# Routing a whole batch row at once, the spread of y about its first channel, and the output matrix's sums inside the first expert, in a fused attention and mixture-of-experts kernel

## The chip, the core and the metric

The kernel runs on one core of a Trainium2 chip. The core's engines each have their own in-order instruction queue: TensorE (PE) multiplies matrices, VectorE (DVE), ScalarE (ACT) and GpSimd (POOL) do elementwise work, and SyncE (SP) issues most DMAs. An engine waits for another through semaphores. SBUF holds the operands, PSUM the products. The metric is the time of one execution in microseconds (us) on the device; lower is better.

## The reference, cut to what is computed

```
x : (4, 1024, 1024) f32, all weights f32
xn  = layernorm(x)                              # no gain, no bias
# attention part
q, v = xn @ Wq, xn @ Wv
s_t  = lam * s_{t-1} + v_t                      # scan over the 1024 tokens, lam per head
y    = layernorm(q * s) * ln_g + ln_b
A    = (y * silu(xn @ Wg)) @ Wo
# experts: 64 experts, the 8 best per token, 128 places per expert
p    = softmax(xn @ router.T)
w, i = top_k(p, 8);  w = w / sum(w)
per expert e, for the first 128 tokens that chose it:
     h = silu(xg @ w1[e].T) * (xg @ v1[e].T)    # 384 wide
     M[token] += w * (h @ w2[e])
out  = x + A + M
```

Tokens are taken for an expert in the order of their position, the four batch rows interleaved.

## The kernel before

**Stages.** `attn_and_routing` works through the four batch rows of 1024 tokens; then `Experts.run` goes through the 64 experts and weaves the 16 products with `Wo` in between them. Within a row, channels lie on the partitions (a "channel block" c is 128 channels; y(c), c = 0 to 7, is one such block of 1024 tokens), and for each m = 0 to 3 there is a product for the states v (`states`), then one for the queries q (`queries`), and after these eight, four products for the gate g (`gates`). Each makes two channel blocks, m and m+4.

**One product.** `steps` (L130 to L175) makes the two channel blocks for all 1024 tokens with seven multiplications of half blocks where the plain way needs eight; each is four matmuls of 128x512. `left_sums` (L49) forms the needed sums of the weights, `right_sums` (L57) those of the right operand: T3, T1, T2, T4 at L61, L64, L66 and L68, in this order; T1 is written over B12. The seven parts lie in PSUM banks of the kinds a, b and c, two of each. ACT copies three of them to SBUF (`sc1`, `sc5`, `sc2`, L148), DVE adds at L160, L169 and L172. Two further banks, t and r, exist once each. In `product` (L178) the last multiplication of one product is left over and is done after two steps of the next one (`before`), and whatever is handed in as `late` comes after five of them.

**Order.** A scheduler chooses each engine's instruction order from the program and its dependences. `in_order` (L79) holds program order on the engines that are named; `keep_in_program_order` pins single instructions. Row 0's preparation is pinned on all engines, experts 0 to 2 on DVE alone (L976).

**Router.** `scored` (L468) makes the logits of half a row (512 tokens): the eight channel blocks of xn are split into two groups of four that are multiplied side by side, 64 experts on partitions 0 to 63 and 64 to 127 of one bank. ACT copies the bank, and `folded` (L487) adds both groups and turns tokens onto the partitions with four matmuls against a constant matrix `fold`. `route` (L501) takes, for 512 tokens, the maximum, the eight best (one MAX8 and one MATCH_REPLACE for each 128 tokens), the softmax over them, and stores the weights to `wtab` in DRAM. Row 0's two halves are scored at the end of its preparation and routed as the function `left` within the first product; the first half of row b+1 is scored and routed after row b's queries m=2, the second before the gates m=3. `take` (L527) turns the selection of each half to experts on partitions (transposes to `sT`, bank r, before the queries m=0) and picks the best 128 tokens for each expert in 16 rounds that are spread over the row.

**Spread of y.** The layernorm of y needs sums over 1024 channels, that is, across partitions and over eight blocks. `sum1` adds the blocks and `sum2` their squares on POOL; a 128x512 matmul with a constant matrix `mean_w` then averages over partitions (`all_channels`). To keep the squares small, the kernel first finds a shift per token from the first two blocks, y(0) and y(4): `find_shift` runs one such matmul per half row inside the product after queries m=0 (as `late`), and `less_shift` subtracts the shift from each block, squares it on ACT (L628 and next) and adds on POOL (L630, L631). `find_spread` runs inside the gates m=0, as `late`: mean matmuls, copies on ACT, the mean's square, the variance matmuls, root and reciprocal.

**Experts.** `hidden` (L883) multiplies the 128 gathered tokens by w1 and v1 (16 matmuls of 128x384) and makes `act`; `output` (L899) turns act (`hpt`, three transposes), copies it (`hT`, L906) and multiplies by w2 (six matmuls of 128x512, `y`). `turned` makes the next expert's transposed tokens `xgT`. `load_wo` (L931) loads the four blocks of Wo and forms their sums, in the program before expert 0; row 3's last gate products are then still running.

Of the kernel before, what the change touches and what calls it, by code (L numbers as in the profile page):

```python
# [8 lines left out]
F32 = mybir.dt.float32  # L9
# [223 lines left out]
def attn_and_routing(  # L233
# [45 lines left out]
    begun = {}  # L279
    first_logits = []  # L280

# [19 lines left out]
    def prep_first():  # L301
# [61 lines left out]
        with in_order(tc):  # L363
            for n in range(4):
                load_x(n)
            load_w(0, (0, 1))
            load_x(4)
            load_x(5)
            load_w(1, (0, 1))
            load_x(6)  # L370
            load_x(7)
            nc.sync.dma_start(out=r_sb, in_=router)
            for w in range(2):
                load_w(w, (2, 3))
            for n in range(3):
                moments(tiles[n], tables[n], f"{n}")
                root_of(n)
                if n > 0:
                    norm(n - 1)
            for n in range(2 * NM):  # L380
                if n > 0:
                    if n + 2 < 2 * NM:
                        moments(tiles[n + 2], tables[n + 2], f"{n + 2}")
                        root_of(n + 2)
                    if n + 1 < 2 * NM:
                        norm(n + 1)
                turn(n)
                for work in then.get(n, ()):
                    work()
            left_sums(nc.vector, ws[0])  # L390
            sums(0)
            left_sums(nc.vector, ws[1])
            halves = [scored(0, h, "rt"[h]) for h in range(2)]
            first_logits.extend(folded(0, h, halves[h], "rt"[h]) for h in range(2))
        begun.update({w: (banks[w, 0], banks[w, 1]) for w in range(2)})
# [71 lines left out]

    def scored(b, h, bank="r"):  # L468


        blocks = quarters[b]
        two = pools.bank(bank, [P, SH], f"lg2_{b}_{h}")
        for k in range(KH):
            for i in range(2):
                nc.tensor.matmul(  # L475
                    two[i * E : (i + 1) * E, :],
                    lhsT=r_sb[:, i * KH + k, :],
                    rhs=blocks[f"B{i + 1}{h + 1}"][:, k, :],
                    start=(k == 0),
                    stop=(k == KH - 1),  # L480
                    tile_position=(0, i * E),
                )
        both = scratch.tile([P, SH], F32, tag="sc", name=f"lgs_{b}_{h}")
        nc.scalar.copy(both, two)
        return both

    def folded(b, h, both, bank="r"):  # L487

        lg = pools.bank(bank, [P, NM, E], f"lg_{b}_{h}")
        for j in range(NM):  # L490
            nc.tensor.matmul(
                lg[:, j, :],
                lhsT=both[:, j * P : (j + 1) * P],
                rhs=fold,
                start=(j == 0),
                stop=(j == NM - 1),
                skip_group_check=True,
            )
        return lg

    def route(b, h, lg):  # L501

        wide = [P, NM, E]
        mx = small.tile([P, NM], F32, tag="mx", name=f"mx_{b}_{h}")
        nc.vector.tensor_reduce(mx, lg, AX.X, ALU.max)
        sh = scratch.tile(wide, F32, tag="sc", name=f"sh_{b}_{h}")
        nc.vector.tensor_tensor(sh, lg, mx.unsqueeze(2).to_broadcast(wide), ALU.subtract)
        nc.vector.tensor_scalar(sh, sh, EXP_MIN, None, ALU.max)
        sel = small.tile(wide, F32, tag="sel", name=f"sel_{b}_{h}")
        for j in range(NM):  # L510
            top = small.tile([P, K], F32, tag="top", name=f"top_{b}_{h}_{j}")
            nc.vector.max(top, sh[:, j, :])
            nc.vector.match_replace(sel[:, j, :], top, sh[:, j, :], TAKEN)
        nc.vector.tensor_tensor(sel, sel, sh, ALU.is_lt)
        nc.scalar.activation(sh, sh, AF.Exp)
        nc.vector.tensor_tensor(sh, sh, sel, ALU.mult)
        sm = small.tile([P, NM], F32, tag="mx", name=f"sm_{b}_{h}")
        nc.vector.tensor_reduce(sm, sh, AX.X, ALU.add)
        nc.vector.reciprocal(sm, sm)
        nc.vector.tensor_tensor(sh, sh, sm.unsqueeze(2).to_broadcast(wide), ALU.mult)  # L520
        r0 = b * S + h * SH
        nc.gpsimd.dma_start(
            out=wtab[r0 : r0 + SH, :].rearrange("(j p) e -> p j e", p=P), in_=sh
        )
        sels[b, h] = sel

    def take(b):  # L527

        cur = one.tile([E, C + S], F32, tag="cur", name=f"cur_{b}")
        for h in range(2):  # L530
            sT = pools.bank("r", [E, SH], f"sT_{b}_{h}")
            for j in range(NM):
                nc.tensor.transpose(
                    sT[:, j * P : (j + 1) * P], sels[b, h][:, j, :], ident
                )
# [46 lines left out]
    def batch_row(b, left):  # L582
# [7 lines left out]

        shift = mean = ys[2][:, 2, :]
        sum1 = one.tile([P, S], F32, tag="sum1", name=f"sum1_{b}")
# [10 lines left out]

        def states(m, left, late):

# [3 lines left out]
            def then(c21):  # L609
# [5 lines left out]
                nc, pools, weights(b, 0, m), quarters[b],  # L615
                lo[:, H0], lo[:, H1], hi[:, H1], then, left, f"v_{b}_{m}", late,
                begun.get(0) if b == 0 and m == 0 else None,
# [3 lines left out]
        def queries(m, lo, hi, left):  # L621
            def less_shift():
                for i, c in enumerate((m, m + KH)):
                    nc.vector.tensor_tensor(y(c), y(c), shift, ALU.subtract)  # L624
                    if m == 0 and i == 0:
                        nc.scalar.activation(sum2, y(c), AF.Square)
                        continue
                    sq = line.tile([P, S], F32, tag="line", name=f"sq_{b}_{c}")  # L628
                    nc.scalar.activation(sq, y(c), AF.Square)
                    nc.gpsimd.tensor_tensor(sum2, sum2, sq, ALU.add)  # L630
                    nc.gpsimd.tensor_tensor(sum1, y(0) if m == 0 else sum1, y(c), ALU.add)  # L631

            def find_shift():
                for h, cols in enumerate((H0, H1)):
                    ps = all_channels(sum1, h, f"sh_{b}_{h}")
                    nc.scalar.activation(shift[:, cols], ps, AF.Copy, scale=float(NM))
                less_shift()

            def then(c21):
                nc.vector.tensor_tensor(y(m + KH, H0), c21, hi[:, H0], ALU.mult)  # L640
                nc.vector.tensor_tensor(y(m), y(m), lo, ALU.mult)
                nc.vector.tensor_tensor(y(m + KH, H1), y(m + KH, H1), hi[:, H1], ALU.mult)
                if m == 0:
                    nc.gpsimd.tensor_tensor(sum1, y(0), y(KH), ALU.add)
                else:
                    less_shift()

# [4 lines left out]
            )  # L652
            return left, find_shift if m == 0 else None

        def find_spread():

            for h, cols in enumerate((H0, H1)):
                ps = all_channels(sum1, h, f"mean_{b}_{h}")
                nc.scalar.copy(mean[:, cols], ps)
            rstd = one.tile([P, S], F32, tag="sum1", name=f"rstd_{b}")  # L660
            nc.scalar.activation(rstd, mean, AF.Square)
            for h, cols in enumerate((H0, H1)):
                ps = all_channels(sum2, h, f"var_{b}_{h}")
                nc.vector.tensor_tensor(rstd[:, cols], ps, rstd[:, cols], ALU.subtract)
            nc.scalar.activation(rstd, rstd, AF.Sqrt, bias=eps)
            nc.vector.reciprocal(rstd, rstd)
            spread.append(rstd)
# [31 lines left out]

        late = None  # L700
        taking = take(b)
        for m in range(NM):
            lo, hi, left = states(m, left, late)
            if b == 0 and m == 0:
# [7 lines left out]
            next(taking)  # L712
            left, late = queries(m, lo, hi, left)
            next(taking)
            if b + 1 < B:
                if m == 1:
                    prep(b + 1, 0)
                elif m == 2:
                    load_turned(b + 1, 0)
                    route(b + 1, 0, folded(b + 1, 0, scored(b + 1, 0)))  # L720
            if m == NM - 1:
# [8 lines left out]
        for m in range(NM):  # L730
            if m == 0 and b + 1 < B:
                prep(b + 1, 1)
            if m == NM - 1 and b + 1 < B:
                load_turned(b + 1, 1)
                route(b + 1, 1, folded(b + 1, 1, scored(b + 1, 1)))
                sums(b + 1)
# [80 lines left out]

    def left():
        for h in range(2):
            route(0, h, first_logits[h])  # L820

    for b in range(B):
# [4 lines left out]
class Experts:  # L827
# [103 lines left out]
    def load_wo(self):  # L931
        for name, (i, o) in zip(("B11", "B21", "B22", "B12"), BLOCKS):
            self.wo_b[name] = self.pools.block(f"wo_{name}")
            load_block(self.nc, self.wo_b[name], self.wo, i, o * SH, SH)
        right_sums(self.nc.vector, self.wo_b, lambda n: self.pools.block(f"wo_{n}"))

# [27 lines left out]
    def run(self):  # L964
        units = B * NM
        gated = self.load_gated(0)
# [7 lines left out]
        for e in range(E):  # L974

            kept = [mybir.EngineType.DVE] if e < 3 else []  # L976
            with in_order(self.tc, kept):
# [3 lines left out]
                if e + 1 < E:  # L981
                    self.turn = self.turned(e + 1)
                if before is not None:
                    self.output(*before)
# [57 lines left out]
```

## Time and profile before

| | us |
|---|---|
| median of three runs | 2669.09 (2668.46 to 2669.94) |
| the profiled execution, its time | 2671.9 |
| its span, first to last instruction | 2670.1 |
| mean granted TensorE clock | 0.997 of full speed |

Some more rows of the page, from its table of the costliest groups. Each gives line, engine and operation, destination and sources with partitions x elements, the count, then busy time in total and the mean in ns of one, then the idle time ahead of them and what ended it.

```profile
L890 PE MATMUL h<-w,xgT 128*128 128x384 f32 x2048 | 672.2, 486 | 0.7 <-issue 0.7
...
L906 DVE COPY hT<-hpt 128x384 f32<-128x384 f32 x64 | 35.6, 557 | 724.5 <-PE hpt L905 724.5
...
L631 POOL TENSOR_TENSOR sum<-sum,y 128x1024 f32<-128x1024 f32 x24 | 56.9, 2373 | 205.2 <-DVE y L624 205.2
```

A f32 matmul shows as two records that overlap in the pipeline, so the mean of one is longer than the distance between their starts; prices are best taken from start to start. A POOL instruction that follows something of DVE shows long idle time, which costs nothing where POOL is not what ends a stage.

The experts take the second half of the span. The attention part ends at about 1255 us, where the first expert's matmuls are already mixed with row 3's last gate product.

### The profile page before, as it was taken

Reading aid. Unit: us, or ns where it says so; the run is one execution under the profiler, and the core shown is the slowest. Engines: PE = TensorE matmul, PEld = TensorE weight load, DVE = VectorE, ACT = ScalarE, POOL = GpSimd, SP = SyncE. Lnnn points to the kernel's source line nnn. Section 1 sums busy time; section 2 is a strip of 40 time slices with the busy share of each in tenths; the row PEclk is TensorE's granted clock in tenths of the full one; section 3 lists DMA queues with packets and bytes.
Section 4 is the critical chain, followed back from the end, with each engine's and each line's share of the span. In section 5 each row is a group of like instructions: output and inputs, shape, how many; then the busy total and the mean of one; then the engine's idle time right before and its main releaser. Section 6 shows DMA issues by size and latency. Waiting matters only on the chain.

```text
span 2670.1 us, 18675 instructions
## 1 busy us (share of the span) xinstructions
PE 2642.0 (99%) x6981; PEld 1272.4 (48%) x6981; DVE 1082.8 (41%) x1426; ACT 330.8 (12%) x492; POOL 737.5 (28%) x655
## 2 busy tenths in 40 slices
PE   9999999999999999999999999999999999999997
PEld 5444444444444444444555555555555555555554
DVE  7945676464943676373222212222122221222221
ACT  4213112131212211121000000000000000000000
POOL 1453312121122102132333323333233332333321
PEclk9999999999999999999999999999999999999999
DMA  6555534443335432326889888898888988889876
GB/s 236 194 182 194 193 107 144 179 156 110 123 110 210 166 116 83 145 98 239 296 284 305 283 274 284 285 304 283 274 284 284 305 283 273 284 286 303 270 272 181
DMA packets 122474, 592.95 MB, mean 222 GB/s; under 512 B 15872, under 2 KB 52736, under 8 KB 89360
## 3 DMA queue, kind: packets, MB, share of 16 engines
q1 hardware_dynamic: 81488, 448.03, 46.1%
q0 software_dynamic: 40464, 143.72, 19.9%
q8 instruction: 55, 0.90, 0.1%
q14 instruction: 35, 0.29, 0.0%
q10 hardware_dynamic: 432, 0.01, 0.0%
HBM read 483.67 MB, written 124.81 MB: 228 GB/s over the span
## 4 chain that ended last, share of the span: by engine, by line
PE 95%; DVE 3%; DMA 1%; issue 0%; ACT 0%; POOL 0%; SPq 0%; POOLq 0%; DVEq 0%; ACTq 0%
PE h L890 25%; PE y L911 12%; PE pa_o L137 8%; PE pa_g L137 8%; PE pa_v L137 7%; PE pa_q L137 7%; PE pc_o L137 4%; PE pc_q L137 4%; PE pc_g L137 4%; PE pc_v L137 4%; PE pb_g L137 2%; PE pb_o L137 2%; PE pb_v L137 2%; PE pb_q L137 2%; PE lg L475 1%; PE hpt L905 1%
## 5 line engine op out<-in xcount | busy, mean ns | idle before, releaser
L890 PE MATMUL h<-w,xgT 128*128 128x384 f32 x2048 | 672.2, 486 | 0.7 <-issue 0.7
L890 PEld LDWEIGHTS h<-w,xgT 128*128 128x128 f32 x2048 | 388.9, 190 | 286.1 <-issue 33.6
L857 POOL DMA_INDIRECT xg<-rows,tables x256 | 252.6, 987 | 669.4 <-DVE xgT L875 603.7
L911 PE MATMUL y<-w,hT 128*128 128x512 f32 x768 | 343.6, 597 | 1.6 <-DVE hT L906 1.6
L906 DVE COPY hT<-hpt 128x384 f32<-128x384 f32 x64 | 35.6, 557 | 724.5 <-PE hpt L905 724.5
L137 PE MATMUL pa_g<-xT,w 128*128 128x512 f32 x512 | 233.9, 600 | 2.9 <-DVE ghi L172 2.9
L911 PEld LDWEIGHTS y<-w,hT 128*128 128x128 f32 x768 | 140.9, 190 | 192.6 <-issue 153.3
L137 PE MATMUL pa_q<-xT,w 128*128 128x512 f32 x480 | 216.5, 593 | 2.0 <-DVE y L172 2.0
L137 PE MATMUL pa_v<-xT,w 128*128 128x512 f32 x480 | 217.4, 593 | 0.0
L137 PE MATMUL pa_o<-wo_T,gated 128*128 128x512 f32 x384 | 177.7, 592 | 0.0
L914 DVE TENSOR_SCALAR ys<-y,wt 128x512 f32<-128x512 f32 x128 | 95.9, 749 | 200.1 <-PE y L911 197.6
L137 PEld LDWEIGHTS pa_g<-xT,w 128*128 128x128 f32 x512 | 97.9, 192 | 127.3 <-issue 123.4
L137 PEld LDWEIGHTS pa_q<-xT,w 128*128 128x128 f32 x480 | 90.6, 190 | 114.6 <-issue 110.5
L137 PEld LDWEIGHTS pa_v<-xT,w 128*128 128x128 f32 x480 | 90.6, 190 | 114.5 <-issue 112.9
L895 ACT ACTIVATE act<-h 128x384 f32<-128x384 f32 x64 | 31.5, 492 | 848.5 <-PE hpt L905 833.2
L922 POOL DMA_INDIRECT out_dram<-ys,tables x63 | 102.5, 1627 | 112.0 <-DMA out_dram<-ohi 83.8
L689 POOL DMA_DIRECT2D gated<-y x64 | 48.2, 758 | 254.1 <-DVE y L684 242.3
L137 PE MATMUL pc_o<-wo_B,gated 128*128 128x512 f32 x256 | 117.1, 592 | 0.0
L137 PE MATMUL pc_g<-xT,w 128*128 128x512 f32 x256 | 115.3, 593 | 1.5 <-ACT sc_g L148 1.5
L137 PE MATMUL pc_v<-xT,w 128*128 128x512 f32 x256 | 115.4, 593 | 0.7 <-ACT sc_v L148 0.7
L137 PE MATMUL pc_q<-xT,w 128*128 128x512 f32 x256 | 115.5, 592 | 0.0
L631 POOL TENSOR_TENSOR sum<-sum,y 128x1024 f32<-128x1024 f32 x24 | 56.9, 2373 | 205.2 <-DVE y L624 205.2
(209 smaller groups left out, 2499.2 us busy)
## 6 DMA issues: line engine op xcount, KB each, us to landing
w<-in_w_dram SPq DMA_DIRECT2D x128, 1536.0 KB
w<-in_v_dram SPq DMA_DIRECT2D x64, 1536.0 KB
w<-wsum SPq DMA_DIRECT2D x36, 1792.0 KB
wsum<-w POOLq DMA_DIRECT2D x12, 1792.0 KB
x<-in_x_dram SPq DMA_DIRECT2D x32, 512.0 KB
rows<-x POOLq DMA_DIRECT2D x32, 512.0 KB
gated<-y POOLq DMA_DIRECT2D x64, 256.0 KB
gated<-gated SPq DMA_DIRECT2D x16, 1024.0 KB
```

The lines of the kernel that those rows point to most:

```text
L137: nc.tensor.matmul(ps, lhsT=lhs[:, slot, k, :], rhs=blocks[right][:, k, :], start=start and k == 0, stop=stop and k == KH - 1, skip_group_ ...
L475: nc.tensor.matmul(two[i * E : (i + 1) * E, :], lhsT=r_sb[:, i * KH + k, :], rhs=blocks[f"B{i + 1}{h + 1}"][:, k, :], start=(k == 0), stop ...
L631: nc.gpsimd.tensor_tensor(sum1, y(0) if m == 0 else sum1, y(c), ALU.add)
L689: nc.gpsimd.dma_start(out=gated[b, :, :, slot, m, :].rearrange("u p j -> p u j"), in_=yc[:, h * SH : (h + 1) * SH].rearrange("p (u j) -> p ...
L857: nc.gpsimd.indirect_dma_start(out=xg[:, r, :], out_offset=None, in_=self.rows.rearrange("n (q c) -> (n q) c", q=NQ), in_offset=bass.Indir ...
L890: nc.tensor.matmul(ps, lhsT=xT[:, k, :], rhs=w[:, k, :], start=(k == 0), stop=(k == KD - 1))
L895: nc.scalar.activation(act, ph[0], AF.Silu)
L905: nc.tensor.transpose(pt[:, j, :], act[:, j * P : (j + 1) * P], self.ident)
L906: nc.vector.tensor_copy(hT, pt)
L911: nc.tensor.matmul(ps, lhsT=hT[:, j, :], rhs=w2[:, j, cols], start=(j == 0), stop=(j == KF - 1))
L914: nc.vector.tensor_scalar(ys[:, cols], ps, wt, None, ALU.mult)
L922: self.nc.gpsimd.indirect_dma_start(out=to, out_offset=bass.IndirectOffsetOnAxis(ap=rows, axis=0), in_=ys, in_offset=None, compute_op=ALU.add,
```

## The change

It has three parts.

1. **Router.** `scored` now makes the logits of a whole row in one bank: 16 matmuls, the two half rows side by side on partitions 0 to 63 and 64 to 127, each summing all eight channel blocks. `by_token` turns the copied bank with four 128x128 transposes in place of the eight `fold` matmuls of a row. For rows 1 to 3 both are in the program before the row before's gates m=3. `route` handles 1024 tokens at once and is called after the states m=0 of the row itself.
2. **Spread.** No shift is found. For each block but the first, `collect` subtracts y(0) into a separate tile `away`, ACT squares it, POOL adds it to sum2, and POOL adds the unshifted block to sum1. `find_spread` corrects sum2 twice: it takes off the square of `off` = sum1 - 8 y(0), which gives the spread about each partition's own mean, and adds the square of sum1/8 - mean, which gives the spread about the mean of all channels. The variance matmuls then go straight into the root.
3. **Experts.** `right_sums` of Wo moves from `load_wo` to the first expert, after the next expert's tokens are turned. Experts 0 to 2 are pinned on DVE and PE.

The core of the diff (`states`, `batch_row` and the loop over rows lose the arguments `late` and `left` that are no longer used):

```diff
-            halves = [scored(0, h, "rt"[h]) for h in range(2)]
-            first_logits.extend(folded(0, h, halves[h], "rt"[h]) for h in range(2))
+            logits[0] = scored(0)
+        logits[0] = by_token(0, logits[0])
...
+    def scored(b):
+        blocks = quarters[b]
+        two = pools.bank("r", [P, SH], f"lg2_{b}")
+        for k in reversed(range(KD)):
+            for h in (1, 0):
                 nc.tensor.matmul(
+                    two[h * E : (h + 1) * E, :],
+                    lhsT=r_sb[:, k, :],
+                    rhs=blocks[f"B{k // KH + 1}{h + 1}"][:, k % KH, :],
+                    start=(k == KD - 1),
+                    stop=(k == 0),
+                    tile_position=(0, h * E),
                 )
+        both = scratch.tile([P, SH], F32, tag="sc", name=f"lgs_{b}")
         nc.scalar.copy(both, two)
         return both
...
+    def by_token(b, both):
+        lg = pools.bank("r", [P, NM, 2 * E], f"lg_{b}")
         for j in range(NM):
+            nc.tensor.transpose(lg[:, j, :], both[:, j * P : (j + 1) * P], ident)
         return lg
...
         def queries(m, lo, hi, left):
+            def collect(c):
+                away = line.tile([P, S], F32, tag="line", name=f"away_{b}_{c}")
+                nc.vector.tensor_tensor(away, y(c), y(0), ALU.subtract)
+                nc.scalar.activation(sum2 if c == KH else away, away, AF.Square)
+                if c != KH:
+                    nc.gpsimd.tensor_tensor(sum2, sum2, away, ALU.add)
+                nc.gpsimd.tensor_tensor(sum1, y(0) if c == KH else sum1, y(c), ALU.add)
...
         def find_spread():
+            off = line.tile([P, S], F32, tag="line", name=f"off_{b}")
+            nc.vector.scalar_tensor_tensor(off, y(0), -float(KD), sum1, ALU.mult, ALU.add)
+            nc.scalar.activation(off, off, AF.Square, scale=KD**-0.5)
+            nc.vector.tensor_tensor(sum2, sum2, off, ALU.subtract)
             for h, cols in enumerate((H0, H1)):
                 ps = all_channels(sum1, h, f"mean_{b}_{h}")
                 nc.scalar.copy(mean[:, cols], ps)
+            nc.vector.scalar_tensor_tensor(off, sum1, 1.0 / KD, mean, ALU.mult, ALU.subtract)
+            nc.scalar.activation(off, off, AF.Square, scale=KD**0.5)
+            nc.vector.tensor_tensor(sum2, sum2, off, ALU.add)
             rstd = one.tile([P, S], F32, tag="sum1", name=f"rstd_{b}")
-            nc.scalar.activation(rstd, mean, AF.Square)
             for h, cols in enumerate((H0, H1)):
                 ps = all_channels(sum2, h, f"var_{b}_{h}")
-                nc.vector.tensor_tensor(rstd[:, cols], ps, rstd[:, cols], ALU.subtract)
-            nc.scalar.activation(rstd, rstd, AF.Sqrt, bias=eps)
+                nc.scalar.activation(rstd[:, cols], ps, AF.Sqrt, bias=eps)
             nc.vector.reciprocal(rstd, rstd)
...
         for m in range(NM):
-            lo, hi, left = states(m, left, late)
+            lo, hi, left = states(m, left)
+            if m == 0:
+                route(b, logits[b])
...
-                    route(b + 1, 0, folded(b + 1, 0, scored(b + 1, 0)))
...
-                route(b + 1, 1, folded(b + 1, 1, scored(b + 1, 1)))
+                logits[b + 1] = by_token(b + 1, scored(b + 1))
...
-        right_sums(self.nc.vector, self.wo_b, lambda n: self.pools.block(f"wo_{n}"))
...
-            kept = [mybir.EngineType.DVE] if e < 3 else []
+            kept = [mybir.EngineType.DVE, mybir.EngineType.PE] if e < 3 else []
             with in_order(self.tc, kept):
                 act = self.hidden(e, self.turn)
...
                 if e + 1 < E:
                     self.turn = self.turned(e + 1)
+                if e == 0:
+                    right_sums(nc.vector, self.wo_b, lambda n: self.pools.block(f"wo_{n}"))
```

## The prediction

> **What bounds the kernel now.** First the page's busy times, then its chain of waits:
>
> ```profile
> PE 2642.0 (99%) x6981; PEld 1272.4 (48%) x6981; DVE 1082.8 (41%) x1426; ACT 330.8 (12%) x492; POOL 737.5 (28%) x655
> ...
> PE 95%; DVE 3%; DMA 1%; issue 0%; ACT 0%; POOL 0%; SPq 0%; POOLq 0%; DVEq 0%; ACTq 0%
> ```
>
> TensorE is the bound. The span is 2670.1 us, so all its waits together are 28.1 us. A part of the change counts only by the TensorE records it takes out or by a TensorE wait it ends or makes; work taken from POOL or ACT is worth nothing by itself. So next the list of waits, engine PE (total, times, longest):
>
> ```profile
> PE pa_g L137 <- DVE ghi L172: 2.9, 1, 2.9
> ...
> PE pc_g L137 <- ACT sc_g L148: 1.5, 1, 1.5
> ...
> PE mean L599 <- POOL sum L631: 0.6, 1, 0.6
> ```
>
> Unit prices come from the TensorE timeline (start, length): a 128x512 f32 matmul is two records and takes 0.86 us (x8 in 3.43 from start to start), a 128x384 one 0.645, a 128x128 transpose 0.109, a pair of 64-wide router matmuls runs side by side at 0.44 each.
>
> **Spread about y(0), what it removes.** Timeline of row 0 after queries m=0:
>
> ```profile
> 94.93 1.02 PE L599 MATMUL sh<-sum,mean_w 128*128 128x512 f32 x2
> 95.79 1.02 PE L137 MATMUL pa_v<-xT,w 128*128 128x512 f32 x2
> 96.65 1.12 PE L599 MATMUL sh<-sum,mean_w 128*128 128x512 f32 x2
> 97.60 2.74 PE L137 MATMUL pa_v<-xT,w 128*128 128x512 f32 x6
> ```
>
> Start to start, 94.93 to 97.60 is 2.67, of which 0.86 is pa_v's own: 1.81 per row, four rows, **-7.25**. The two ACT shift copies and two of POOL's 15 adds (2.35 each) go too; both engines have room there: nothing.
>
> **Router of a row at once.** Row 0's second router half for row 1, at gates m=3:
>
> ```profile
> 310.20 1.07 PE L475 MATMUL lg<-xT,r_sb 128*64 128x512 f32 x2
> 311.20 1.13 PE L137 MATMUL pb_g<-xT,w 128*128 128x512 f32 x2
> 312.17 2.74 PE L137 MATMUL pa_g<-xT,w 128*128 128x512 f32 x6
> 314.91 3.65 PE L475 MATMUL lg<-xT,r_sb 128*64 128x512 f32 x14
> 318.49 1.12 PE L137 MATMUL pa_g<-xT,w 128*128 128x512 f32 x2
> 319.45 1.00 PE L491 MATMUL lg<-fold,lgs 128*128 128x64 f32 x8
> ```
>
> 310.20 to the next product at 320.29 is 10.09, less ten product records at 0.43: 5.80, of which the lone lg is 1.0 and the fold block 0.94. The first half, in one piece (173.17 to 176.85), costs 3.68 and its fold block 0.94. Together 10.42 per row. After: 16 matmuls in an unbroken run, which row 0 does in 7.02 before, 0.3 for two switches, four transposes 0.44, 0.15 hand-over: 7.9. Three rows: **-7.6**. Row 0 has the long run already and only swaps two fold blocks (1.88) for transposes (0.55): **-1.3**. If the scheduler splits the new run as it split the old one, 1.1 a row is lost again.
>
> route() of rows 1 to 3 now falls after states m=0, on DVE, of which 41% is busy; about 12 us of it stand before sel (16 rounds at 0.325 each way, 256- and 512-wide operations at 0.42 and up). The instruction order by engine puts the selection transposes sT some 48.8 us after the logits' last product and sel 41.8 after it: nothing, with 7 us to spare. In row 0, sel is ready at about 55.1 where PE comes at 54.5, because one L169 and one 2.2 scan stand in front of its last rounds: 0.75, less 0.2 of a wait that goes, **+0.55**. DMAs: the same two wtab stores per row on POOL's queue, later but long before the experts gather from them; SP's order is the same in both programs.
>
> Row 0's wait of pc_v for sc_v (0.66 idle, 0.82 start to start) stood behind the old MAX8 rounds: **-0.8**.
>
> **Sums of Wo inside the first expert.** PE first, then DVE at that place:
>
> ```profile
> 1248.27 6.66 PE L137 MATMUL pa_g<-xT,w 128*128 128x512 f32 x8 [2.90 <-DVE ghi L172]
> ```
>
> ```profile
> 1242.53 2.29 DVE L61 TENSOR_TENSOR wo_T<-wo_B,wo_B 128x2048 f32<-128x2048 f32 x1 [10.23 <-DMA wo_B<-in_wo_dram]
> 1244.73 0.68 DVE L169 TENSOR_TENSOR glo<-pc_g,sc_g 128x512 f32<-128x512 f32 x1
> 1245.33 2.28 DVE L64 TENSOR_TENSOR wo_B<-wo_B,wo_B 128x2048 f32<-128x2048 f32 x1
> 1247.53 0.69 DVE L172 TENSOR_TENSOR ghi<-pa_g,sc_g 128x512 f32<-128x512 f32 x1
> ```
>
> DVE stood idle 10.23 us for the last block of Wo, with L169 and L172 of the gate product queued behind its sum, and PE waited for L172. The sums now come behind xgT of expert 1, so the wait goes: 3.07 from start to start. The x8 behind it took 6.66 instead of 3.43 to 3.65; 3.07 more. **-6.14**. What is late next is the first experts' own chain. PE's order is now pinned for e<3 (DVE's alone before), so the three transposes hpt and y come in program order, with none of the 28 h matmuls or of pa_o moved between. e=0's h0 of expert 1 waits as before, without hpt in it: +0.33. e=1: act 0.55, xgT 1.24 and hT 0.52 stand on DVE between the last h and the first y; 2.24 by their pitches and hand-overs (0.15 each). e=2 has one pa_o part between: 1.72. Sum **+4.3**. In before the pa_o x6 at 1276.27 covered it. The sums of Wo themselves (4 x 2.29 on DVE) lie beside the h matmuls of expert 1 (20.6 us); their DMA, whose last part lands near 1242, is no longer waited for.
>
> **Spread, what it adds.** find_spread runs inside gates m=0 between two steps of a product. Before it, the mean matmuls stood first. Now DVE's `off`, ACT's Square of it and DVE's subtraction stand in front of the copies that release PE. Each queue is in order, so: rows 1 and 2: the Square of off precedes sc5_g, for which pc_g's next product waits; row 3: it precedes sc2_g, for which T3's product waits; row 0: mean_1 shares the one bank "r" with mean_0, whose copy stands behind Square, table load (1.28) and a silu. Row 0's old waits (1.48 and 0.56, 244.7 and on) stay.
>
> How late is off? This is the widest unknown. Below, 1.33, a free 1024-wide L684 row; above, the remains of POOL's last add (2.35) and then 1.33. The rows with both engines at work:
>
> ```profile
> 146.70 3.31 DVE L578 TENSOR_TENSOR_SCAN lo<-lam,lo 128x1024 f32<-128x1024 f32 x1
> ```
>
> ```profile
> 146.60 1.27 POOL L52 TENSOR_TENSOR w<-w 128x512 f32<-128x512 f32 x1
> 147.82 3.25 POOL L53 TENSOR_TENSOR w<-w 128x512 f32<-128x512 f32 x1
> ```
>
> Alone the scan takes 2.38 and POOL's sum 1.27: each was held by the other, nearly for its whole length. So off, two SBUF inputs, that is ready in the same instant as POOL's sum2+=away_7, starts behind it. The Trainium skill says the same and more sharply (SBUF — State Buffer, "Who interferes with whom"): a DVE instruction with two SBUF operands and POOL exclude each other for a whole instruction. It speaks against this change: by the free row the chain off (1.33), Square (1.06), sc copy (0.59) fits nearly inside the products' slack, by the lock it doesn't:
> - rows 1, 2: +2.1 each (near 0 free)
> - row 0: +2.2 (1.1 free)
> - row 3: POOL has eight gathers of experts 0 and 1 (10.25 us) in front of its last adds, and one DVE away (1.15) pushes the table chain; mean_0 +1.5, T3's wait +4.45 (2.3 free), and the clock.
>
> The clock: the windows view (us, then busy of PE, PEld, DVE, ACT, POOL, the granted clock PEclk, DMA share, GB/s) says what a wait of 2.90 does afterwards:
>
> ```profile
> 1248.30:1255.00 6.70, 6.70 (x9) 2.88 (x10) 5.61 (x3) 0.61 (x2) 1.50 (x2) 0.56 0.19 78
> ```
>
> and after 1.48 idle at 244.7 the next x8 took 3.67 at clock 1.00. So the edge lies between 1.5 and 2.9. The skill (TensorE: Matmul & The Clock Gate, Part 1) puts it at an idle window of about 3.4 us that runs freely, a longer limit than this row shows. By the page neither the 2.1s nor 2.9 would fall; by the row 2.9 did, and 2.1 to 2.24 may. I take both as safe, 2.1 as nearer 1.48 and 2.24 as midway with the page's longer limit behind it, and row 3's 4.45 as lost by both: +3.07. Row 3 is then 9.0 (4.8 free: 1.5, 2.3 and half a loss, 0.95).
>
> Sum 2.1 + 2.1 + 2.2 + 9.0 and 0.2 of later var waits: **+15.6** (6.5 free). The off Square on ACT before var is otherwise hidden by the gates' products.
>
> **Sum.** -7.25 -7.6 -1.3 -0.8 -6.14 = -23.1; +0.55 +4.3 +15.6 = +20.45; net **-2.65**. The profiled run took 2671.9 (span 2670.1, 1.8 about it), 2.8 over the median of 2669.09; the difference is taken to the median: **2666.4**. Differences under 0.2% (5.3 us) can't be told from no change here: below 2663.8 counts as faster, above 2674.4 as slower.
>
> **Rivals.**
> 1. Forecast, 0.40: held off, as summed; its own range 2662 to 2671 (each of the five new waits a fifth off).
> 2. Off isn't held, 0.30: POOL's last add falls before or after it, as its start depends on one hand-over. Spread costs 6.5: net -12, **2657**. For it: the scan row is one whose POOL partner had started 0.1 us earlier. Against: off and the add are released by nearly the same events.
> 3. Slower, 0.18: the clock falls after each wait of 2.1 to 2.24, not only after row 3's. Places: gates m=0 of rows 0 to 2, h0 of expert 1, y of experts 0 and 1; 3.07 each, six of them 18.4: **2685**. One is enough to pass the old time (2669.4), three to pass 2674.4. For it: 2.90 fell. Against: 1.48 didn't.
> 4. Route comes late, 0.12: whole-row sel isn't ready at sT in rows 1 to 3 as in row 0, for DVE takes scans and loads first; about 2 us in four rows: **2674.5**. Against: 7 us to spare.
>
> Below 2663.8: nearly all of case 2 (0.29) and 0.05 of case 1: 0.34, taken as 0.33. Above 2674.4: case 3 (0.18), half of case 4 (0.06), 0.03 of case 1: 0.27. Between: 0.40. The range, 2655 to 2681, leaves out the low end of case 2 and the upper end of case 3.
>
> **What will show it.** No sh rows; in rows 1 to 3 one run of 32 lg records of 7 us and four transposes: else the router term is off. The pa_g row behind the gates' last product with no wait for ghi and clock 1.00. New waits in PE's list: y for hT (2.2 and 1.7), pc_g for sc_g near 2 in two rows, pa_g for sc_g near 4.5 in row 3 with a granted clock near 0.5 behind it, mean for an ACT copy in row 0, sT for sel once, 0.75. On DVE, off longer than 1.33 where POOL adds beside it; 1.33 there means case 2. A granted clock under 1 after the 2.2 waits means case 3; sT waits in each row, case 4. Wrong altogether I am if the scheduler fills the pinned expert chain by other means or if a weight load now lands late.

## The result and the profile after

| | before | after |
|---|---|---|
| median of 20 runs, us | 2669.45 (2666.95 to 2670.91) | 2673.74 (2671.83 to 2676.01) |
| ratio after/before | | 1.0018, 95% interval 1.0012 to 1.0025 |
| profiled execution, time / span | 2671.9 / 2670.1 | 2673.46 / 2671.5 |
| TensorE busy | 2642.0 | 2629.5 |
| span less TensorE busy | 28.1 | 42.0 |

The changed kernel is slower by 4.3 us. The effect is small, but the interval leaves out 1. TensorE lost 12.5 us of records and gained 13.9 us of waits. The page's busy times and the first line of its chain, after:

```profile
PE 2629.5 (98%) x6917; PEld 1265.5 (47%) x6917; DVE 1103.7 (41%) x1398; ACT 313.1 (12%) x472; POOL 744.5 (28%) x647
...
PE 91%; DVE 5%; issue 1%; POOL 1%; ACT 1%; DMA 1%; POOLq 0%; DVEq 0%; ACTq 0%
```

In the chain TensorE's share fell from 95% to 91%; DVE, issue, POOL and ACT took the difference. A busy share of 98% conceals part of the loss, for a matmul at a slow clock counts as busy too. The list of waits names the places (total, times, longest; one line that is the same before is left out at the dots):

```profile
PE pc_g L137 <- ACT sc_g L148: 4.6, 3, 1.5
PE y L902 <- DVE hT L897: 4.4, 3, 2.8
PE h L881 <- issue: 4.3, 2, 2.4
PE pa_q L137 <- DVE y L172: 4.0, 3, 2.0
PE pa_g L137 <- ACT sc_g L148: 3.8, 1, 3.8
...
PE mean L596 <- POOL sum L626: 1.8, 2, 1.2
PE mean L596 <- ACT y L652: 1.7, 1, 1.7
PE sT L530 <- DVE sel L509: 1.1, 1, 1.1
```

The wait of pa_g for ghi (2.9) is gone. In its place stand three waits in the first experts (h twice, y), two more of pc_g for sc_g, one of pa_g for sc_g, and in row 0 one of pa_q for y. The router came out as one piece. TensorE's timeline in row 0's gates m=3:

```profile
309.61 7.09 PE L475 MATMUL lg<-xT,r_sb 128*64 128x512 f32 x32
316.62 1.12 PE L137 MATMUL pa_g<-xT,w 128*128 128x512 f32 x2
317.58 0.60 PE L491 MATMUL lg<-ident,lgs 128*128 128x128 f32 x4
```

From 309.61 to the next product at 318.02 is 8.41, less 0.86 of product: 7.55 per row where 10.42 stood before. The scores of rows 2 and 3 take 8.42 in the same form.

**Row 1's spread.** Four views of the changed kernel, the timelines of DVE, POOL, ACT and TensorE (start, length, then what it waited for):

```profile
540.68 3.36 DVE L647 SCALAR_TENSOR_TENSOR off<-y,sum 128x1024 f32<-128x1024 f32 x1 [2.60 <-POOL sum L626]
```

```profile
540.61 2.34 POOL L625 TENSOR_TENSOR sum<-sum,away 128x1024 f32<-128x1024 f32 x1
```

```profile
544.07 1.06 ACT L648 ACTIVATE off<-off 128x1024 f32<-128x1024 f32 x1 [6.81 <-DVE off L647]
545.04 0.57 ACT L148 COPY sc_g<-pc_g 128x512 f32<-128x512 f32 x1
```

```profile
545.66 3.70 PE L137 MATMUL pc_g<-xT,w 128*128 128x512 f32 x8 [1.54 <-ACT sc_g L148]
```

Off is issued 0.07 after POOL's addition and ends 1.1 after it; its length is POOL's 2.34 and about one free duration (1.21, see the run without POOL's addition). The copy of pc_g had its product soon after 540.5, but stands behind the Square in ACT's queue, and TensorE goes on only at 545.66. In row 3 the same kind of wait is longer, and the eight records behind it take 6.03 from start to start where 3.43 is normal:

```profile
1161.54 6.19 PE L137 MATMUL pa_g<-xT,w 128*128 128x512 f32 x8 [3.83 <-ACT sc_g L148]
```

**Row 0's query product.** TensorE needs the bank that DVE's L172 reads. First DVE and TensorE after, then DVE and TensorE before:

```profile
129.85 0.68 DVE L172 TENSOR_TENSOR y<-pa_q,sc_q 128x512 f32<-128x512 f32 x1
```

```profile
130.59 3.70 PE L137 MATMUL pa_q<-xT,w 128*128 128x512 f32 x8 [2.04 <-DVE y L172]
```

```profile
129.03 0.67 DVE L172 TENSOR_TENSOR y<-pa_q,sc_q 128x512 f32<-128x512 f32 x1
```

```profile
131.08 3.60 PE L137 MATMUL pa_q<-xT,w 128*128 128x512 f32 x8
```

Before, L172 ended 1.4 ahead of TensorE. Now TensorE is ready at 128.4, 2.7 earlier than before, and L172 comes 0.8 later; the slack has turned into a wait.

**First experts.** TensorE's timeline after, then DVE and ACT between the last h and the first y:

```profile
1258.12 12.25 PE L881 MATMUL h<-w,xgT 128*128 128x384 f32 x32 [1.92 <-issue]
1270.21 0.49 PE L896 MATMUL hpt<-ident,act 128*128 128x128 f32 x3
1273.47 5.42 PE L902 MATMUL y<-w,hT 128*128 128x512 f32 x12 [2.77 <-DVE hT L897]
...
1299.35 0.49 PE L896 MATMUL hpt<-ident,act 128*128 128x128 f32 x3
1302.21 0.88 PE L881 MATMUL h<-w,xgT 128*128 128x384 f32 x2 [2.37 <-issue]
1302.93 7.01 PE L902 MATMUL y<-w,hT 128*128 128x512 f32 x12
```

```profile
1271.26 0.55 DVE L887 TENSOR_TENSOR act<-act,h 128x384 f32<-128x384 f32 x1 [4.09 <-ACT act L886]
1271.74 1.24 DVE L866 STREAM_TRANSPOSE xgT<-xg 128x1024 f32<-128x1024 f32 x1
1272.90 0.52 DVE L897 COPY hT<-hpt 128x384 f32<-128x384 f32 x1
```

```profile
1270.74 0.49 ACT L886 ACTIVATE act<-h 128x384 f32<-128x384 f32 x1 [19.17 <-PE hpt L896]
```

Before, six records of pa_o stood in the same gap:

```profile
1265.88 10.56 PE L890 MATMUL h<-w,xgT 128*128 128x384 f32 x32 [0.65 <-issue]
1276.27 2.74 PE L137 MATMUL pa_o<-wo_B,gated 128*128 128x512 f32 x6
1278.85 5.32 PE L911 MATMUL y<-w,hT 128*128 128x512 f32 x12
```

The profile gives no releaser for the two h waits ("issue"); DVE's xgT ended about 0.1 before each.

Besides the three waits, two blocks are longer than their kind: h x32 takes 12.09 from start to start (10.32 elsewhere) and y x12 takes 6.84 (5.15). The windows view (us, busy of PE, PEld, DVE, ACT, POOL, then the granted clock, DMA share, GB/s) shows why:

```profile
1255.34:1258.75 3.41, 1.49 (x5) 0.68 (x4) 2.44 (x3) 0.00 (x0) 0.45 (x1) 1.00 0.93 317
1258.75:1262.16 3.41, 3.41 (x7) 1.71 (x6) 3.38 (x2) 0.00 (x0) 3.10 (x2) 0.50 0.99 418
1302.90:1306.00 3.10, 3.10 (x5) 1.20 (x4) 0.00 (x0) 0.00 (x0) 2.38 (x3) 0.54 0.86 334
```

A clock of 0.5 follows the waits of 1.92 and 2.37 and, in row 3 (0.50 from 1161.50 to 1165.00), that of 3.83 us. Behind the wait of 2.77 none is lost (5.25 for y x12).

### The profile page after: what moved, and what is told of

Its sections match the earlier page's. It is cut to its first block, busy times and chain, and to the rows that moved or that the text cites. A ratio compares the mean times of both kernels' runs of the same rounds, so it can differ in the third digit from the quotient of the medians.

```text
span 2671.5 us, 18489 instructions
## 1 busy us (share of the span) xinstructions
PE 2629.5 (98%) x6917; PEld 1265.5 (47%) x6917; DVE 1103.7 (41%) x1398; ACT 313.1 (12%) x472; POOL 744.5 (28%) x647
## 4 chain that ended last, share of the span: by engine, by line
PE 91%; DVE 5%; issue 1%; POOL 1%; ACT 1%; DMA 1%; POOLq 0%; DVEq 0%; ACTq 0%
PE h L881 24%; PE y L902 13%; PE pa_o L137 8%; PE pa_g L137 7%; PE pa_v L137 7%; PE pa_q L137 7%; PE pc_o L137 4%; PE pc_v L137 4%; PE pc_q L137 4%; PE pc_g L137 3%; PE pb_o L137 2%; PE pb_g L137 2%; PE pb_q L137 2%; PE pb_v L137 2%; PE lg L475 1%
## 5 line engine op out<-in xcount | busy, mean ns | idle before, releaser
L626 POOL TENSOR_TENSOR sum<-sum,y 128x1024 f32<-128x1024 f32 x24 | 71.5, 2978 | 273.3 <-DVE y L630 231.3
```

The source lines that it names most:

```text
L626: nc.gpsimd.tensor_tensor(sum1, y(0) if c == KH else sum1, y(c), ALU.add)
```

## The experiments

Each run's ratio is against the kernel before on the same chip, with its 95% interval. A gain over the changed kernel is a difference of medians; taken through the ratios, these gains come out within 1.3 us of the ones given.

**The three parts, each alone, and the kernel before once more.** The first has only the router's part of the diff (`scored`, `by_token`, `route`, `take` and their calls), the second only that of `states`, `queries` and `find_spread`, the third only the lines below:

```diff
-        right_sums(self.nc.vector, self.wo_b, ...)          # in load_wo
...
-            kept = [mybir.EngineType.DVE] if e < 3 else []
+            kept = [mybir.EngineType.DVE, mybir.EngineType.PE] if e < 3 else []
...
+                if e == 0:
+                    right_sums(nc.vector, self.wo_b, ...)
```

> The kernel before with the router part alone. From the two traces: router work of rows 1 to 3 falls by 10.42 - 7.55 = 2.87 each (-8.6), row 0's fold blocks -1.3, the waits of sT for sel cost 1.25 + 3 x 0.3: -7.75, so 2661.7 (ratio 0.9971). Rival: the 2.0 us wait of row 0's q product for DVE (new in the changed kernel) comes from the later route, not from the spread: 2663.1 and the wait pa_q <- y of 2.0 in the list.

> The kernel before with the spread about y(0) alone. Shift matmuls -7.25; find_spread +1.84 + 2 x 1.71 + 8.1 = +13.4 if the off chain costs the same as in the changed kernel: +6.1, 2675.5 (ratio 1.0023). If the 2.0 us wait of row 0's q product belongs to this part, +7.5, 2676.9. Rival: row 3's 8.1 needs the three parts together (POOL's gathers stand elsewhere): -2, 2667.

> The kernel before with the sums of Wo inside the first expert and the pinning of TensorE alone. The prediction's terms (-6.14 + 4.3) give 2667.6. The traces' waits with their clock losses (+11.0 in place of 1.75, so +9.25, against -6.14) give +3.1: 2672.5. If the clock loss of 3.07 behind the old wait happens only in some executions of the kernel before, the median gains less: up to 2675.

> The kernel before, unchanged: 2669.4, ratio 1.000. Its times lie in two groups about 3 us apart (2666.9 to 2668.5 and 2669.1 to 2670.9). If the groups are executions without and with the clock loss behind the 2.9 us wait, this profile shows either 6.66 for the eight pa_g records and a time near 2670.5, or 3.4 to 4 and a time near 2667.5. Rival: the loss is in every execution and the groups come from elsewhere: 6.66 with a time near 2667.5, or 3.5 near 2670.5.

| | median us | ratio |
|---|---|---|
| router alone | 2662.61 | 0.9975 (0.9966 to 0.9985) |
| spread alone | 2677.04 | 1.0029 (1.0017 to 1.0040) |
| expert part alone | 2675.44 | 1.0023 (1.0015 to 1.0031) |
| kernel before again | 2669.99 | 1.0002 (0.9993 to 1.0010) |

The router gains about 6.9 us; the other two lose 7.6 and 6.0. Their sum, +6.6, is above the measured +4.3, but each of the three is known only to 2 to 3 us, so an interaction isn't shown. The expert part lies well above my prediction's -1.8 for it, and a little above the 2675 that the expectation allowed. Row 3's long wait (3.82, with 2.1 of clock behind it) is there with the spread alone, so it doesn't need the other parts. The router alone has row 0's q wait (1.80), the spread alone has it not, but a pc_v wait of 2.43 instead of 0.66; DVE is late in row 0 in either form.

The expectation on the two groups of times fell. Behind the same wait for ghi the profile of the kernel before, taken again, shows another clock than the first (0.56), and with the spread alone none is lost. The windows view of the kernel before again, then of the spread alone:

```profile
1249.10:1254.30 5.20, 5.20 (x8) 2.20 (x9) 5.17 (x3) 0.61 (x1) 1.49 (x2) 0.67 0.25 101
```

```profile
1254.90:1258.40 3.50, 3.48 (x8) 1.63 (x9) 3.46 (x3) 0.63 (x1) 1.50 (x2) 1.00 0.19 77
```

The eight pa_g records lost 3.07, 1.81 and 0.1 after waits of 2.90, 2.83 and 2.45. So the loss differs between executions (the last section says on what it hangs); but this second profile belongs to a time of 2671.67, not to one of the shorter ones, so what sorts the times into groups stays open.

**TensorE's order in the first experts freed.**

```diff
-            kept = [mybir.EngineType.DVE, mybir.EngineType.PE] if e < 3 else []
+            kept = [mybir.EngineType.DVE] if e < 3 else []
```

> The changed kernel with the first three experts pinned on DVE alone, as before; Wo's sums stay inside the first expert. If the pinned order of TensorE makes the new waits (h 1.92 and 2.37, y 2.77, with clock losses 1.77 and 1.69), they go down to the 1.75 of the kernel before: -9 to -10, 2664. Rival: Wo's sums on DVE in front of act and hT make them, whatever TensorE's order: 2671 to 2673.

2664.24, ratio 0.9980 (0.9972 to 0.9988): 9.5 better than the changed kernel, as expected. TensorE's timeline in this run, the same place as above:

```profile
1258.40 0.55 PE L896 MATMUL hpt<-ident,act 128*128 128x128 f32 x3 [0.72 <-DVE act L887]
1259.61 10.56 PE L881 MATMUL h<-w,xgT 128*128 128x384 f32 x32 [0.65 <-issue]
1270.00 2.74 PE L137 MATMUL pa_o<-wo_B,gated 128*128 128x512 f32 x6
1272.58 5.32 PE L902 MATMUL y<-w,hT 128*128 128x512 f32 x12
```

hpt goes ahead of expert 1's h, and six records of pa_o cover act, xgT and hT. All three long waits and both clock losses are gone, while Wo's sums still run on DVE in the same place (1259.43 to 1268.66). So the pinning of TensorE was the loss, not the moved sums.

**ACT in program order in the gates m=0.**

```diff
-            return product(...)
+            with in_order(tc, [mybir.EngineType.Activation] if m == 0 else []):
+                return product(...)
```

> The changed kernel with ACT held to program order in the gates m=0, which puts sc5 and sc2 in front of the Square of off. The waits of pc_g in rows 1 and 2 (1.71 each) and of pa_g in row 3 (4.09 and 2.60 of clock) go: -10.1, 2663.6. Rival: in row 3 the second mean matmul then waits for the first mean's copy, which still stands behind off, its Square and the table load, as in row 0 (1.84): about 3 come back, 2666.6. If the lateness of off itself held the engines elsewhere: no change.

2669.11, ratio 1.0000 (0.9992 to 1.0009): 4.6 better, less than half of what was expected. The waits for sc_g in rows 1 and 2 and in row 3 are gone, but the rival came true in row 3, on TensorE and then on ACT:

```profile
1161.72 1.94 PE L596 MATMUL mean<-sum,mean_w 128*128 128x512 f32 x2 [3.41 <-ACT y L652]
```

```profile
1157.12 1.06 ACT L648 ACTIVATE off<-off 128x1024 f32<-128x1024 f32 x1 [7.37 <-DVE off L647]
...
1161.10 0.57 ACT L652 COPY y<-mean 128x512 f32<-128x512 f32 x1
```

The copy of the first mean, which frees bank r, now stands behind the Square, a table load and a silu (the dots). 1.8 of clock is lost behind this wait.

**Means before off, ACT in program order.** This adds to the edit above:

```diff
         def find_spread():
+            for h, cols in enumerate((H0, H1)):
+                ps = all_channels(sum1, h, f"mean_{b}_{h}")
+                nc.scalar.copy(mean[:, cols], ps)
             off = line.tile([P, S], F32, tag="line", name=f"off_{b}")
             nc.vector.scalar_tensor_tensor(off, y(0), -float(KD), sum1, ALU.mult, ALU.add)
             nc.scalar.activation(off, off, AF.Square, scale=KD**-0.5)
             nc.vector.tensor_tensor(sum2, sum2, off, ALU.subtract)
-            for h, cols in enumerate((H0, H1)):
-                ps = all_channels(sum1, h, f"mean_{b}_{h}")
-                nc.scalar.copy(mean[:, cols], ps)
```

> As the run with ACT in program order, and off is computed after the copies of the mean, so that no copy that TensorE waits for stands behind it. All of find_spread's new waits go but row 3's 1.41 for POOL's sum1: 13.4 - 1.4 = -12, 2661.7. Rival: the later root (Sqrt and Silu tables now take turns on ACT) comes too late for the first gate product's normalisation, and the gain shrinks to that of the run with ACT in program order.

2664.29, ratio 0.9978 (0.9969 to 0.9987): 9.4 better than the changed kernel, where 12 was expected. find_spread's new waits shrink to 1.41 in row 0 and 1.40 and 1.16 in row 3. Off is still 3.36 long in rows 1 to 3, and the copies that TensorE waits for no longer stand behind it. Whether the means first, without ACT in program order, would do the same was not tried.

**No POOL addition beside off.**

```diff
+                if c == KD - 1:
+                    last.append(away)
-                if c != KH:
+                elif c != KH:
                     nc.gpsimd.tensor_tensor(sum2, sum2, away, ALU.add)
...
+            nc.vector.tensor_tensor(sum2, sum2, last[0], ALU.add)
             nc.vector.tensor_tensor(sum2, sum2, off, ALU.subtract)
```

> The changed kernel with the last addition to sum2 (channel block 7) on DVE behind off instead of on POOL, so that POOL adds nothing while off runs; ACT's order is as in the changed kernel. If DVE and POOL exclude each other, off takes 1.33 instead of 3.36 and 2.27: pc_g's waits in rows 1 and 2 go to near 0 (-3.4), row 3's pa_g wait is 2 shorter, row 0's mean wait 1 shorter: -6 to -9 with the clock, 2665 to 2668. Rival: off is long by itself (it reads a tile that POOL has just written): off stays above 3 and the time at 2673.7.

2669.72, ratio 1.0004 (0.9995 to 1.0012): 4.0 better, where 6 to 9 was expected. DVE and POOL in row 1:

```profile
538.37 3.37 DVE L651 TENSOR_TENSOR sum<-sum,away 128x1024 f32<-128x1024 f32 x1 [2.63 <-POOL sum L627]
...
542.26 1.21 DVE L649 SCALAR_TENSOR_TENSOR off<-y,sum 128x1024 f32<-128x1024 f32 x1
```

```profile
538.31 2.34 POOL L628 TENSOR_TENSOR sum<-sum,y 128x1024 f32<-128x1024 f32 x1
```

Off is 1.21 with POOL idle, so it isn't long by itself. But the scheduler put the new addition ahead of off, and it is now this one that is held for 3.37 by POOL's last sum. The wait of pc_g falls from 1.54 to 0.96 only. The mutual exclusion is shown (off 3.36 beside POOL's addition, 1.21 without it); its removal took only a third off the wait in rows 1 and 2, since what it held up was only replaced. In row 3 the wait fell from 3.83 to 1.70, with no clock lost behind it, but row 0 got a new wait of 1.50 before its first variance matmul.

**Repairs together.** The first keeps router and moved sums (pinned on DVE alone) with the spread of before; the second has all three parts, with the freed TensorE order and the means before off; the third adds the edit without POOL's addition.

> The kernel before with the router part and with Wo's sums inside the first expert, pinned on DVE alone (the spread as before, with its shift). From the router alone (2662.6) the wait of 2.9 and its clock loss (1.8 to 3.1) go: -4.9, 2657.7. Rival: without the pinned TensorE order the experts' start costs as much as it saves: 2662.6.

> The changed kernel with both repairs: experts pinned on DVE alone, and in the gates m=0 ACT in program order with off after the means. The two gains stand at different places, so they add: 2673.7 - 9.5 - 9.4 = 2654.8, which beats both kernels; the spread about y(0) is then worth 2.9 against the run without it (2657.7). Rival: the spread is worth nothing even so, 2657.7 or more.

> As the run with both repairs, with the last addition to sum2 on DVE behind off. If TensorE no longer waits for anything behind off, the exclusion of DVE and POOL costs nothing there: 2654.8, same as that run within 1, although off is 1.2 instead of 3.36. Rival: off's lateness still costs elsewhere (the variance and the root): 2 less.

| | median us | ratio |
|---|---|---|
| router, moved sums, spread of before | 2658.52 | 0.9962 (0.9948 to 0.9975) |
| all three, repaired | 2653.82 | 0.9942 (0.9928 to 0.9955) |
| the same, last addition on DVE | 2652.19 | 0.9936 (0.9923 to 0.9950) |

These came within 3 us of what was expected. The repaired change beats both kernels, by 15.5 us (12 to 19) against before. Comparing the first two, the spread about y(0) looks worth 4.7 once its order is mended, but the intervals of these two overlap, and in their profiles 3.7 of the difference stands in row 0's q product (a wait of 2.87 with 1.8 of clock behind it in the first, 1.01 with none in the second). How much is the spread's own stays open. In the third the wait of row 3's second mean (1.17) is gone, but its 1.6 is within the intervals.

## Why the prediction was wrong

I forecast -2.65 against the profiled run and 2666.4; the profiled runs give +1.6 and the medians +4.3. The time lies inside the range, the sign is wrong. The terms, each from start to start in the two profiles:

| term | forecast | measured |
|---|---|---|
| shift matmuls | -7.25 | -7.25 |
| router, rows 1 to 3, and row 0 | -8.9 | -9.9 |
| the wait for ghi and its clock | -6.14 | -6.14 |
| row 0: sT, pc_v, q | -0.25 | +2.3 |
| experts 0 to 2 | +4.3 | +9.25 |
| find_spread | +15.6 | +13.4 |

What is left, 0.3 for sT in each of rows 1 to 3 and 0.95 of a wait of kq that is gone, cancels.

**The step that failed is the experts' term, +4.3, which measured +9.25.** Both halves of it were named and then mis-sized: the waits by 1.5 and the clock, put at nothing, by 3.46. The waits: I put act, xgT and hT between the last h and the first y, 2.24; it is 2.93, for act is two instructions, ACT's silu (0.49) and DVE's product (0.55), and only one was in the sum. In expert 2 it is 2.53 for 1.72, for the same reason, and a pair of h records stands in the gap where I had put a part of pa_o. The clock: I took waits up to 2.24 as safe, from one wait of 1.48 without loss and the Trainium skill's longer limit. In the profile 1.92 and 2.37 lost 1.77 and 1.69. Expert 0's wait is not even a new one: before, the same 2.08 from start to start had three hpt transposes in its middle and lost nothing; undivided it fell to half speed here, though only in two of five profiles. Freeing TensorE's order took 9.5 us off, so this term is enough to turn the sign. The third rival had named this mechanism, at six places and 3.07 each; two of them, at under 1.8, were enough with the rest.

**Row 0.** The q product's wait for DVE (2.04, 2.21 with hand-over) was not foreseen: I took what TensorE saves ahead of this place as gained, and did not ask whether DVE keeps up. The wait is in the router alone too, and between 1.0 and 2.9 in the other runs with that part. Part of its size is one scan ahead of L172 on DVE: 2.28 beside POOL's additions in the changed kernel, 1.26 in the run with all three parts repaired, where the wait is 1.01.

**The way from profile to median.** I took the difference in the profile over to the median. The first profile of the kernel before was 2.5 above the median of the 20 runs, that of the changed kernel 0.3 below; this makes 2.7 of the 7.3 us by which the forecast missed. A part of it can be the clock loss of 3.07, a size that was 1.81 when the same kernel was profiled again. So the exact agreement of the -6.14 is no merit: it was read from that one execution.

**What held.** The router's term, the shift's, and find_spread's in kind and place, with sizes near the forecast: rows 1 and 2 at 1.71 (forecast 2.1), row 0's mean at 1.84 (2.2), row 3 at 8.1 with its half-speed clock (9.0), and off held for POOL's addition (3.36). The second rival, off unheld, is excluded by its rows. Late route (fourth rival) showed in row 0 alone: 1.25 for sel, 0.3 in the others.

## What to carry to other kernels

Take the chain behind a TensorE wait from the queues instruction by instruction. Then ask of each wait of about 2 us or more whether it could fall into one window of the clock (below), and add half a window as a chance; work that fills part of the wait makes this less likely. Where TensorE is relieved ahead of a place at which another engine is close behind, count only the slack of that engine as gained. Pinning an order that the scheduler had been filling with other products needs a price for each product that leaves the gap. Where a long elementwise step is added beside a matmul loop, see that the small copies which free the PSUM banks stand ahead of it in their engine's queue: here that was worth 9.4 us, and a shorter step 4.0.

## What was unexpected of the hardware

The clock loss is no fixed function of the wait. Over the profiles of these runs waits of up to 1.80 lost nothing; 1.92 lost 1.77 in two executions and nothing in three; 2.04, 2.06 and 2.43 nothing; 2.37 lost 1.7 to 1.8 in all five; 2.45 lost 0.1; 2.53 lost nothing once and 1.8 once; 2.77 lost nothing in three and 1.5 and 1.8 in two; 2.83 to 2.95 lost 1.8 in three and 3.07 in one; 3.41 lost 1.8; 3.82 to 3.83 lost 2.1 to 2.7.

The clock records kept in the 13 traces give the order in this. Every stretch between two changes of the clock is a whole multiple of 3.413 us, so each trace has a fixed grid of such windows. I took from the matmul records how long TensorE stood idle in each window. All 18 falls to half speed ahead of the end of the kernel come at the end of a window with 1.92 us or more of idle time. Every window at full speed with 2.06 or more was followed by a fall, none with 1.80 or less was, and 1.92 in one window fell in two cases of three. The windows view on this grid, the kernel before and then the spread alone:

```profile
1244.02:1247.43 3.41, 1.35 (x5) 0.47 (x3) 3.41 (x3) 1.06 (x1) 0.00 (x0) 1.00 0.62 256
1247.43:1254.26 6.83, 5.99 (x7) 2.52 (x8) 6.47 (x5) 0.63 (x1) 1.50 (x2) 0.50 0.19 77
```

```profile
1249.99:1253.40 3.41, 2.48 (x7) 0.95 (x5) 3.41 (x3) 1.06 (x1) 0.00 (x0) 1.00 0.88 364
1253.40:1256.81 3.41, 1.89 (x5) 0.93 (x6) 3.41 (x4) 0.63 (x1) 0.44 (x1) 1.00 0.01 2
```

The wait of 2.90 had 2.06 in one window, and the clock fell; that of 2.45 was cut by the grid into 0.93 and 1.52, and it didn't. A slow stretch lasts one window, or two where TensorE is still idle for 0.84 us or more in the first (0.55 and less: one). Half of TensorE's busy time in it is 1.4 to 1.7 for one window and 2.1 to 3.0 for two, within 0.1 of the losses. So whether a wait of 1.92, 2.53 or 2.77 us cost anything here was the luck of the grid.

The Trainium skill (TensorE: Matmul & The Clock Gate, Part 1) calls the window of about 3.4 us free-running and the warm-up different from run to run; the grid of 3.413 us agrees with the first. Its "≥1 idle window" as the condition for the fall does not: a window idle for 2.06 of its 3.41 us was enough.
